# First edges of a graph layer: the sources' exponentials taken from the gathered rows, head by head, on ScalarE

## The chip, the cores and the metric

The kernel runs on one core of one Trainium2 chip. The metric is the time of one execution on the device in microseconds (us); for the kernel before it is the median of 3 runs. Engine names follow the profile: PE is the matrix engine (TensorE), DVE VectorE, ACT ScalarE, POOL GpSimd, and SP the engine that issues most plain DMAs.

## What is computed

The layer has 6250 nodes of 256 features and three parts. The change lies in the first, attention over 200,000 edges that are sorted by destination, with four heads of 64:

```
z  = einsum('ni,hid->nhd', h, W)
es = einsum('nhd,hd->nh', z, a_src)
ed = einsum('nhd,hd->nh', z, a_dst)
e  = es[src] + ed[dst];  e = where(e >= 0, e, 0.01 * e)
alpha = exp(e - max over dst) / sum over dst
out = segment_sum(alpha[:, :, None] * z[src], dst)
```

The second part (the mixer) is a linear attention over all nodes: x @ Wqkv, an exponential softmax of q and k, a 256x256 context, an output product and a norm. The third is a feed-forward part of four experts, whose gate is a second edge attention (131,072 edges). `x` plus the first two, normed, is the input of the third.

## The kernel before, in words

The exponential of a leaky sum is the larger of two products: exp(e) is max(exp(es) exp(ed), exp(0.01 es) exp(0.01 ed)), each up to a shift. So a source has eight factors, four heads by two slopes, and a destination eight; an edge's weight is the larger of two products for each head. `source_factors` and `factors_of` (L211 to L214) make the sources' ones: the largest term of each head, `most_1`, is subtracted, and two activations follow, one with a bias of 60 (`shift_c`) and one with the scale 0.01.

The program has these stages. **Head:** the nodes are normed and projected; each node's row of z with its four terms es (264 numbers, `ztab`) goes to DRAM, and the largest es of each head over all nodes becomes `most_1` (a tile of 128x4). **First edges:** the edges are laid out in 1612 chunks of 128, 33 for each tile of 128 destination nodes (28 for the last). Eight chunks are a group; there are 202 groups, the last with four chunks. **Second edges** with the feed-forward part follow, with 784 gathers from another table (L1321).

A group of first edges passes through these methods of `FirstEdges`:

- `gather` (L784, POOL): eight indirect DMAs, one for each chunk, bring 128 rows of `ztab` each into `gt` tiles of four chunks. There are seven such tiles, so three and a half groups.
- `sources` (L798, L213, L214): on DVE, for each of the two `gt` tiles, the four terms of each chunk minus `most_1`, into `src_d` (128x16); then on ACT two activations over the whole group (128x32) into `src_f`.
- `load`, `one_hot` (L807, L813), `one_hot_t` (L822), `terms` (L828, PE) and `terms_sum` (L836): the destination's factors, by a one-hot product.
- `weights` (L840, L842, DVE): the eight products and the larger of each pair, into a PSUM tile `dv`. L840 is the only reader of `src_f`.
- `weigh` (L848, DVE): the gathered rows of four chunks times the weights, in place.
- `add` (L857, PE): each chunk's one-hot matrix times its weighed rows, summed in PSUM per destination tile; a finished tile goes through `node_sums` (L766 to L768).

The order is written out by hand, in a loop over groups: gather of group g+2, `weights` and first half of `weigh` of g, `terms` of g+1, first half of `add` of g, second half of `weigh`, `one_hot` of g+1, second half of `add`, `one_hot_t` of g+2, `terms_sum` and `sources` of g+1. Between these, at six slots, `mix_hops` issues the next steps of the mixer and of the second norm (L172, L179, L883, L921, L959 to L981), which go PE, ACT, PE, DVE in turn, and at the end of each round comes one step of a sort for the second edges (L381, L383). A scheduler then places the instructions, mostly in this order, and each engine carries out its own in the order so fixed. It also adds the semaphore waits: before an instruction that reads a gathered tile, one for each of the tile's four landings; before a gather into a tile, the tile's former users.

Of the kernel before, what the change touches and what calls it, by code (L numbers as in the profile page):

```python
# [9 lines left out]
F32 = mybir.dt.float32  # L10
# [3 lines left out]
AF = mybir.ActivationFunctionType  # L14
OP = mybir.AluOpType
# [5 lines left out]
P = 128  # L21
# [6 lines left out]
G1 = 8  # L28
GH = 4
K1, K1L = 33, 28  # L30

ZW = 4 * 65
# [11 lines left out]
SHIFT = 60.0  # L44
# [15 lines left out]
def rows(t):  # L60
    return min(P, N - t * P)
# [3 lines left out]
def gps_layer(ctx: ExitStack, tc: tile.TileContext, a: dict, out: bass.AP):  # L65
    nc = tc.nc
    V, S, G, T, SP = nc.vector, nc.scalar, nc.gpsimd, nc.tensor, nc.sync
# [51 lines left out]
    ek = first.enter_context(tc.tile_pool(name="ek", bufs=1))  # L119
    pw3 = ek.tile([P, NB, 24], BF16, name="pw3")  # L120
    most_1 = ek.tile([P, 4], F32, name="most_1")


    def root(pool, var, n, w, tag):
# [70 lines left out]
    def source_max(pool, ps, m2, es, tag):  # L195

        m1 = pool.tile([P, 4], F32, name=tag + "_m1")
        V.tensor_reduce(m1, es.rearrange("p t h -> p h t"), AX.X, OP.max)
        V.tensor_copy(m2, max_over_partitions(pool, ps, m1, 4, tag))
# [12 lines left out]
    def factors_of(src_f, d, slope):  # L212
        S.activation(src_f[:, :, 0:4], d, AF.Exp, bias=shift_c)  # L213
        S.activation(src_f[:, :, 4:8], d, AF.Exp, scale=slope)  # L214

    def dest_factors(dst_f, u, ed, m2, slope):

        V.tensor_add(u[:, :, 4:8], ed, m2[:, None, :].to_broadcast([P, NT, 4]))
        V.tensor_scalar(u[:, :, 0:4], u[:, :, 4:8], 0.0, 1.0 - slope, op0=OP.min, op1=OP.mult)
        V.tensor_scalar(u[:, :, 4:8], u[:, :, 4:8], 0.0, slope - 1.0, op0=OP.max, op1=OP.mult)  # L220
        S.activation(dst_f[:, :, 0:4], u[:, :, 0:4], AF.Exp)
        S.activation(dst_f[:, :, 4:8], u[:, :, 4:8], AF.Exp, bias=shift_c)

    def in_three(parts, f, r):

        V.tensor_copy(parts[:, :, 0:8], f)
        V.tensor_sub(r, f, parts[:, :, 0:8])
        V.tensor_copy(parts[:, :, 8:16], r)
        V.tensor_sub(r, r, parts[:, :, 8:16])
        return V.tensor_copy(parts[:, :, 16:24], r)  # L230
# [268 lines left out]
    with tc.tile_pool(name="a_x", bufs=1) as ax, tc.tile_pool(name="a_w", bufs=3) as aw, tc.tile_pool(  # L499
        name="a_p", bufs=2, space=PSUM  # L500
# [242 lines left out]
    with tc.tile_pool(name="s1_w", bufs=1) as w, tc.tile_pool(name="s1_p", bufs=1, space=PSUM) as ps:  # L743
        df = q_2[:, : NT * 8].rearrange("p (t f) -> p t f", f=8)
        source_max(w, ps, most_1, es_all[:, :, 0:4], "f1")
        dest_factors(df, dl_2[:, : NT * 8].rearrange("p (t h) -> p t h", h=8), es_all[:, :, 4:8], most_1, 0.01)
        V.memset(pw3, 0.0)
        head_end = in_three(pw3[:, :NT], df, dl_2[:, : NT * 8].rearrange("p (t f) -> p t f", f=8))
    V.memset(h_all[:, NT - 1, :], 0.0)
# [20 lines left out]
    class FirstEdges:  # L770
# [20 lines left out]
        def sources(self):  # L791

            n = self.n
            d = self.w.tile([P, G1, 4], F32, name="src_d", bufs=1)
            self.sf = self.w.tile([P, G1, 8], F32, name="src_f")
            for c0 in range(0, n, GH):
                c1 = min(c0 + GH, n)
                V.tensor_sub(  # L798
                    d[:, c0:c1], self.gt[c0 // GH][:, : c1 - c0, ZW:], most_1[:, None, :].to_broadcast([P, c1 - c0, 4])
                )  # L800
            factors_of(self.sf[:, :n], d[:, :n], 0.01)

        def load(self, rows_):

# [231 lines left out]
    with tc.tile_pool(name="g1_w", bufs=2) as w, tc.tile_pool(name="g1_g", bufs=7) as gp, tc.tile_pool(  # L1036
        name="m_w", bufs=2
# [78 lines left out]
    with tc.If(many != 0):  # L1116
# [7 lines left out]
        with tc.tile_pool(name="sl_k", bufs=1) as k, tc.tile_pool(name="sl_w", bufs=1) as w, tc.tile_pool(  # L1124
            name="sl_p", bufs=1, space=PSUM
# [80 lines left out]
            for t in range(NT):  # L1206
                n, n0 = rows(t), t * P
# [30 lines left out]
    with tc.tile_pool(name="d_k", bufs=1) as dk:  # L1238
# [3 lines left out]
        with tc.tile_pool(name="d_o", bufs=1) as do:  # L1242
# [5 lines left out]
            with tc.tile_pool(name="s2_p", bufs=1, space=PSUM) as ps1:  # L1248
                room = acc2.rearrange("p t f -> p (t f)")
                source_max(do, ps1, most_2, h_all[:, :, HW:HF], "f2")  # L1250
                d = room[:, : NT * 4].rearrange("p (t h) -> p t h", h=4)
# [454 lines left out]
        with tc.tile_pool(name="g2_w", bufs=2) as w, tc.tile_pool(name="g2_g", bufs=6) as gp, tc.tile_pool(  # L1706
            name="g2_p", bufs=1, space=PSUM
# [88 lines left out]
        with tc.If(bad != 0):  # L1796

            own_edges()
            with tc.tile_pool(name="h2_k", bufs=1) as hk, tc.tile_pool(name="h2_w", bufs=1) as w, tc.tile_pool(
                name="h2_p", bufs=1, space=PSUM  # L1800
# [60 lines left out]
```

## Time and profile before

| | us |
|---|---|
| median of 3 runs | 3219.29 (3212.33 to 3220.07) |
| the profiled execution | 4023.54 |
| its span, first to last instruction | 4021.7 |
| first gather of the first edges (L784) starts | 138.1 |
| last gather of the first edges starts | 2614.0 |
| first and last gather of the second edges (L1321) | 2642.2 and 3957.9 |
| busy in the span: PE, DVE, ACT, POOL | 2498.4, 2464.6, 506.5, 2328.2 |

The profiled execution takes a quarter longer than a run. In its span there are stretches in which several engines start nothing, and many waits are put down to "remote", which means that the releaser is not in the profile.

How to read the lines. In a list of groups a line names its line of code, engine and operation, what is written and read, the shapes and a count; then the busy time and the mean duration in ns, then the idle time of the engine ahead of it and what ended most of it. In a timeline a line begins with its start and its duration, and ends, in brackets, with the idle time before it and the releaser. "issue" is idle time for which the profile shows no wait. In a list of waits a line gives who waited for whom, the sum in us, how often, and the longest. A queue entry is a wait that the engine's sequencer carries out; it is not counted as busy.

### The profile page before, as it was taken

Reading aid. Unit: us, or ns where it says so; the run is one execution under the profiler, and the core shown is the slowest. Engines: PE = TensorE matmul, PEld = TensorE weight load, DVE = VectorE, ACT = ScalarE, POOL = GpSimd, SP = SyncE. Lnnn points to the kernel's source line nnn. Section 1 sums busy time; section 2 is a strip of 40 time slices with the busy share of each in tenths; the row PEclk is TensorE's granted clock in tenths of the full one; section 3 lists DMA queues with packets and bytes.
Section 4 is the critical chain, followed back from the end, with each engine's and each line's share of the span. In section 5 each row is a group of like instructions: output and inputs, shape, how many; then the busy total and the mean of one; then the engine's idle time right before and its main releaser. Section 6 shows DMA issues by size and latency. Waiting matters only on the chain. (4 is left out here: it accounts for less than half of the span.)

```text
span 4021.7 us, 36890 instructions
## 1 busy us (share of the span) xinstructions
PE 2498.4 (62%) x10919; PEld 1773.3 (44%) x10920; DVE 2464.6 (61%) x6571; ACT 506.5 (13%) x1319; POOL 2328.2 (58%) x2436
## 2 busy tenths in 40 slices
PE   5666677755564555546555555446666767677766
PEld 4444565544443444434444433324444444444444
DVE  5566666677774776766677566625555546565657
ACT  2200011111110110111111111121111011111112
POOL 2466666665665666656666566655556556555552
PEclk8778798877776777777777777767888788888878
DMA  5443344444443443444444444332222123222221
GB/s 166 131 114 109 108 116 110 119 119 116 122 130 97 116 123 108 120 112 115 133 116 127 113 125 109 104 81 51 45 60 50 42 49 81 53 61 57 59 56 32
DMA packets 248565, 388.33 MB, mean 97 GB/s; under 512 B 73447, under 2 KB 156279, under 8 KB 248090
## 3 DMA queue, kind: packets, MB, share of 16 engines
q0 software_dynamic: 103296, 230.96, 23.1%
q1 hardware_dynamic: 142893, 154.04, 12.6%
q8 instruction: 91, 1.49, 0.1%
q14 instruction: 129, 1.05, 0.1%
q10 hardware_dynamic: 2156, 0.80, 0.1%
HBM read 345.44 MB, written 40.15 MB: 96 GB/s over the span
## 5 line engine op out<-in xcount | busy, mean ns | idle before, releaser
L784 POOL DMA_INDIRECT gt<-ztab,src_c x1612 | 1551.5, 962 | 967.3 <-issue 406.3
L857 PE MATMUL ag<-gt,oh 128*128 128x260 f32 x3224 | 1017.2, 474 | 342.6 <-DVE gt L848 232.0
L1321 POOL DMA_INDIRECT gt<-htab,src x784 | 748.6, 955 | 595.3 <-DVE dv L1390 261.2
L857 PEld LDWEIGHTS ag<-gt,oh 128*128 128x128 f32 x3224 | 754.0, 241 | 527.2 <-DVE gt L848 255.0
L1427 PE MATMUL hp<-xy,w 128*128 128x512 f32 (+1 forms) x832 | 444.3, 657 | 187.2 <-ACT hT L1432 140.5
L1447 PE MATMUL yo<-w,hT 128*128 128x256 f32 x1568 | 446.4, 425 | 111.4 <-issue 63.8
L848 DVE TENSOR_TENSOR gt<-gt,dv 128x1040 f32<-128x1040 f32 x403 | 489.0, 1224 | 13.7 <-issue 12.6
L1447 PEld LDWEIGHTS yo<-w,hT 128*128 128x128 f32 x1568 | 316.5, 209 | 246.2 <-issue 137.2
L883 PE MATMUL m<-wqkv,xy 128*128 128x256 f32 (+1 forms) x784 | 254.6, 464 | 169.5 <-DVE kmax L894 85.3
L1427 PEld LDWEIGHTS hp<-xy,w 128*128 128x128 f32 x832 | 169.0, 216 | 328.5 <-issue 167.3
L883 PEld LDWEIGHTS m<-wqkv,xy 128*128 128x128 f32 (+1 forms) x784 | 171.8, 231 | 217.2 <-DVE kmax L894 91.3
L813 DVE TENSOR_TENSOR oh<-dv,dl_c 128x1024 f32<-128x1024 f32 x202 | 244.0, 1208 | 7.8 <-PE ag L857 5.2
L1432 ACT ACTIVATE hT<-hp,b 128x512 f32<-128x512 f32 (+1 forms) x208 | 133.5, 660 | 479.4 <-remote 172.9
L1371 DVE TENSOR_TENSOR e_sel<-ed,ohq 128x384 f32<-128x384 f32 x98 | 54.1, 552 | 182.4 <-remote 136.8
L213 ACT ACTIVATE src_f<-src_d,shift_c 128x32 f32<-128x32 f32 x202 | 64.9, 321 | 772.5 <-DVE src_d L798 441.4
L381 DVE MAX8 src<-dl 128x8 f32<-128x1024 f32 x128 | 155.5, 1215 | 0.0
L383 DVE MATCH_REPLACE8 dl<-src,dl 128x1024 f32<-128x1024 f32 x127 | 153.5, 1209 | 0.0
L976 PE MATMUL m<-m_sb,qT 128*128 128x256 f32 (+1 forms) x196 | 74.4, 516 | 125.4 <-ACT qT L973 86.8
L1412 DVE TENSOR_REDUCE ag<-ag 128x40 f32<-128x120 f32 x98 | 27.2, 277 | 193.5 <-remote 154.5
L828 PE MATMUL ed<-pw,ohT 128*128 128x24 bf16 x1612 | 71.8, 176 | 106.7 <-DVE ohT L822 46.3
L828 PEld LDWEIGHTS <-ohT 128*128 128x128 bf16 x1612 | 67.1, 100 | 141.6 <-DVE ohT L822 53.6
L836 DVE TENSOR_REDUCE pw<-ed 128x64 f32<-128x192 f32 x202 | 69.6, 344 | 94.9 <-remote 74.6
(374 smaller groups left out, 2745.7 us busy)
## 6 DMA issues: line engine op xcount, KB each, us to landing
br<-rows SPq DMA_DIRECT2D x299, 256.0 KB
gt<-ztab,src_c POOLq DMA_INDIRECT x1612
gt<-htab,src POOLq DMA_INDIRECT x784
early<-ys SPq DMA_DIRECT2D x24, 512.0 KB
ys<-early SPq DMA_DIRECT2D x24, 512.0 KB
ztab<-zt SPq DMA_DIRECT2D x48, 132.0 KB
row<-in_x_dram SPq DMA_DIRECT2D x48, 128.0 KB
out_dram<-ys SPq DMA_DIRECT2D x47, 128.0 KB
```

The lines of the kernel that those rows point to most:

```text
L381: V.max(out=srtf[:, 8 * i : 8 * i + 8], in_=keyf)
L383: V.match_replace(out=keyf, in_to_replace=srtf[:, 8 * i : 8 * i + 8], in_values=keyf, imm_value=0.0)
L784: G.indirect_dma_start(out=self.gt[-1][:, c % GH, :], out_offset=None, in_=ztab[:, :], in_offset=bass.IndirectOffsetOnAxis(ap=self.idx[:, ...
L813: V.tensor_tensor(self.oh[:, :n], self.dv[:, None, :P].to_broadcast([P, n, P]), self.dl[:, :, None].to_broadcast([P, n, P]), op=OP.is_equal,)
L828: T.matmul(self.ed[:, c, :], self.ohT[:, c * P : (c + 1) * P], pw3[:, ds(self.tiles[c], 1), :].rearrange("p a b -> p (a b)"), start=True, ...
L848: V.tensor_mul(gz, gz, self.wp[:, c0:c1].unsqueeze(3).to_broadcast([P, c1 - c0, 4, 65]))
L857: T.matmul(sums[t], self.oh[:, c], self.gt[c // GH][:, c % GH, 0:ZW], start=(s0 + c == 0 or chunk_tile[s0 + c - 1] != t), stop=last,)
L883: T.matmul(out_, xy[:, t, j, :n], wqkv[:, j, c0 : c0 + D], start=(j == 0), stop=(j == 1))
L1321: G.indirect_dma_start(out=self.gt[:, c, : tab.shape[1]], out_offset=None, in_=tab[:, :], in_offset=bass.IndirectOffsetOnAxis(ap=self.idx[ ...
L1427: T.matmul(hp[:, :m], wts[e][0][:, c, j * P : (j + 1) * P], xy[:, t0 : t0 + nt, c] if m == nt * P else xy[:, t0, c, :m], start=(c == 0), s ...
L1432: S.activation(h[:, :m], hp[:, :m], AF.Gelu, bias=b1[:, e, j : j + 1])
L1447: T.matmul(yo[:n], hT[j][:, o : o + n], wts[e][1][:, j, :], start=(j == 0 and e < EARLY), stop=(j == 3))
```

## The change

The subtraction ahead of the exponentials goes. The largest terms are folded into biases, made once: `less_1` (128x8) holds 60 - most_1 for the four factors of slope 1 and -0.01 most_1 for the four of slope 0.01. In `sources`, ACT reads the terms straight from the gathered tile, at a stride of one row of 264, one activation for each tile, head and slope: 16 activations of 128x4 elements for a group instead of two of 128x32, and no DVE operation. `src_d` is gone. Nothing else is edited; `factors_of` stays in use for the second edges.

```diff
+    less_1 = ek.tile([P, 8], F32, name="less_1")
...
         dest_factors(df, dl_2[:, : NT * 8].rearrange("p (t h) -> p t h", h=8), es_all[:, :, 4:8], most_1, 0.01)
+        V.tensor_scalar(less_1[:, 0:4], most_1, -1.0, SHIFT, op0=OP.mult, op1=OP.add)
+        V.tensor_scalar(less_1[:, 4:8], most_1, -0.01, None, op0=OP.mult)
...
         def sources(self):
 
             n = self.n
-            d = self.w.tile([P, G1, 4], F32, name="src_d", bufs=1)
             self.sf = self.w.tile([P, G1, 8], F32, name="src_f")
             for c0 in range(0, n, GH):
                 c1 = min(c0 + GH, n)
-                V.tensor_sub(
-                    d[:, c0:c1], self.gt[c0 // GH][:, : c1 - c0, ZW:], most_1[:, None, :].to_broadcast([P, c1 - c0, 4])
-                )
-            factors_of(self.sf[:, :n], d[:, :n], 0.01)
+                for f in range(8):
+                    es = self.gt[c0 // GH][:, : c1 - c0, ZW + f % 4]
+                    S.activation(
+                        self.sf[:, c0:c1, f], es, AF.Exp, bias=less_1[:, f : f + 1], scale=1.0 if f < 4 else 0.01
+                    )
```

## The prediction, made before the change was run

> **What bounds the kernel now.** The page first. Its group list names the two gathers as the largest POOL work:
>
> ```profile
> L784 POOL DMA_INDIRECT gt<-ztab,src_c x1612 | 1551.5, 962 | 967.3 <-issue 406.3
> ...
> L1321 POOL DMA_INDIRECT gt<-htab,src x784 | 748.6, 955 | 595.3 <-DVE dv L1390 261.2
> ...
> L213 ACT ACTIVATE src_f<-src_d,shift_c 128x32 f32<-128x32 f32 x202 | 64.9, 321 | 772.5 <-DVE src_d L798 441.4
> ```
>
> One mean per gather (962 ns) does not say at what pace POOL can go, so the second view is the timeline of POOL alone:
>
> ```profile
> 1001.19 0.94 POOL L784 DMA_INDIRECT gt<-ztab,src_c  x1 [0.30 <-issue]
> 1002.44 0.94 POOL L784 DMA_INDIRECT gt<-ztab,src_c  x1 [0.30 <-issue]
> 1003.69 0.95 POOL L784 DMA_INDIRECT gt<-ztab,src_c  x1 [0.30 <-issue]
> ...
> 1016.21 0.94 POOL L784 DMA_INDIRECT gt<-ztab,src_c  x1 [0.30 <-issue]
> 1020.53 0.94 POOL L784 DMA_INDIRECT gt<-ztab,src_c  x1 [3.37 <-DVE qm L959]
> ```
>
> Two gathers that wait for nothing start 1.25 us apart. Over the first edges I took all start-to-start distances from the trace: 1400 of 1611 lie near 1.254, and the other 211 carry 453 us above that. At L1321, 71 distances carry 334 us more. If no gather waited, the profiled execution would be: 138 us to the first gather, 1611 x 1.254 + about 3 = 2023, 28 to the first of the second edges, 783 x 1.252 + 1 = 982, 64 to the end: 3235, with the 1.8 us around the span 3237. The profiled execution itself took 4023.54 us (span 4021.7). The median of the runs is 3219.29. So 3237 misses the median by 0.6%, and 4024 misses it by 25%: the runs look like the profile with POOL never held up. I take POOL's pace, 8 x 1.254 = 10.03 us per group of 8 chunks, as the bound of both edge stages. The consumers of a group must then need less than 10.03 us.
>
> Do they? From 440 to 2540 us the stretches show a mean of 201 us of DVE in 300, 67%. There are 201 group periods in 2466 us, 12.27 each, so DVE is busy 8.2 us a group and PE (176 of 300) 7.2. Third, the periods from one L840 to the next: taking out every gap of over 0.8 us in which DVE, ACT and PE all start nothing leaves 8.7 us, taking out only those over 1.5 us leaves 9.8. The 39 groups with no such gap have a median of 8.3. Margin under POOL: 0.2 to 1.7 us. This margin decides the case.
>
> Fourth, the step that changes, in the timeline of all engines:
>
> ```profile
> 1000.43 0.42 ACT L963 ACTIVATE kq<-kq 128x256 f32<-128x256 f32 x1 [2.71 <-DVE kq L962]
> ...
> 1004.74 0.25 DVE L798 TENSOR_TENSOR src_d<-gt,most 128x16 f32<-128x16 f32 x2
> ...
> 1005.08 0.32 ACT L213 ACTIVATE src_f<-src_d,shift_c 128x32 f32<-128x32 f32 x1 [4.23 <-DVE pw L836]
> 1005.31 0.21 ACT L214 ACTIVATE src_f<-src_d 128x32 f32<-128x32 f32 x1
> 1006.04 0.20 DVE L840 TENSOR_TENSOR pw<-pw,src_f 128x64 f32<-128x64 f32 x1
> ...
> 1022.03 0.42 ACT L963 ACTIVATE kq<-kq 128x256 f32<-128x256 f32 x1 [9.35 <-DVE kq L962]
> ...
> 1025.37 0.21 DVE L840 TENSOR_TENSOR pw<-pw,src_f 128x64 f32<-128x64 f32 x1
> ```
>
> and the waits of DVE:
>
> ```profile
> DVE pw L840 <- ACT src_f L214: 45.5, 10, 18.5
> ...
> DVE src_d L798 <- DMA gt<-ztab,src_c: 8.6, 3, 4.9
> ```
>
> ACT stands idle before L213 because it waits for the subtraction; DVE hardly waits for ACT, and in this execution hardly for a gather.
>
> **The change, part by part.**
>
> Removed, DVE: 403 subtractions (two a group, one in the last). A pair holds DVE from 1004.74 to the next start at 1004.90, 0.16 us, elsewhere 0.22: 0.19 x 202 = 38 us. What hides it: POOL's 10.03. Worth 0 while POOL bounds; without that cover 38 us.
>
> Removed, ACT: 404 activations over 32 elements, together about 0.35 us of ACT a group (0.228 from the first start to the second, 0.12 to whatever follows it).
>
> Added, ACT: 201 x 16 + 8 = 3224 activations over 4 elements, each with a bias from a tile. The nearest row is the square root over 4 elements with such a bias, L126, 297 ns by itself. For a row of them only L213 followed by another shows the distance: 0.228 us over 32 elements. The 256- and 32-element exponentials (415 and 321) are not alike in bias, so for the size I take the 297 against 321 of the bias rows: 0.228 - 0.024 = 0.204. Sixteen take 16 x 0.204 + 0.09 = 3.35 us; if nothing overlapped, 16 x 0.297 = 4.75. I take 3.35, since consecutive ones do overlap in the trace. ACT gains 3.0 us a group, 606 us in all; it was busy 36 of 300, so 1.5 us a group, and comes to 4.5 of 10.03. Not a bound; at 4.75 it would be 5.9.
>
> A rule speaks against the split: the Trainium skill, "Perfetto Trace Analysis", section Optimizing Scalar/DVE Operations, gives a fixed overhead of about 93 ns per ScalarE operation on SBUF and advises larger operations where the engine is saturated. By that figure 14 more operations are, as an estimate, 1.3 us a group; by the row they are 3.0. I use the row. With either, ACT stays far from full (at most 45%), and the time would be 3220; by the rule's figure the lateness below would halve.
>
> What is late: L840 needs the last of the sixteen. They depend on the gathers and no longer on DVE, so they can start when ACT's earlier work is done. In the first example ACT is free at 1000.85, done by 1004.2, before L840 at 1006.04: no delay. In the second it is free at 1022.45, done at 1025.8, against L840 at 1025.37: 0.4 late. Doing this comparison for all 202 groups, L840 is late in 74, on the mean over all 0.63 us; the next ACT operation is late by 0.16. Queued behind the sixteen on ACT are the mixer's copies and exponentials (L922, L963, L973, L978, L173), for which PE waits. Together 0.8 us a group, less the 0.19 of DVE: +0.6. The lower end is -0.5: L840's waits for ACT (45.5 + 17.2 of issue, 0.31 a group) vanish if the activations run early, and the 0.19. Either way 8.3 to 8.7 becomes 8.9 to 9.3, under 10.03: worth 0 here.
>
> Waits that move: the four landings of each tile, awaited by L798 (806 queue waits for 403 tiles), are now awaited by ACT, and by the in-place multiply L848 too, just where L798 stood ahead of it. A gather has to wait for ACT's reads as well: one more queue entry per tile at POOL. Its price is bounded by what POOL shows: a gather with one such entry ahead that was not held starts 1.254 us after the last, as without, and the one at L1321 with three starts after 1.249. The entries run under the gather before. I take 0; 43 ns x 403 = 17 us if one were exposed. ACT is never the tile's last reader: its reads end before L840, the PE reads that free the tile come after. So a tile comes free later by the 0.6 above at most, and the 7 tiles, 3.5 groups of gathers, cover that.
>
> A second rule bears on the removal: the skill's "GPSIMD Engine Reference", section Key points, says that GpSimd shares its SBUF interfaces with VectorE and contends with instructions of two SBUF inputs. L798 is one. By the rule at its strongest its 403 x 0.166 = 67 us could come off POOL. The row says otherwise: beside L848, 1.23 us with two SBUF inputs at 1001.79, the gathers keep 1.25. I take 0.
>
> Two small DVE operations ahead of the stage: about 0.15 each, beside the gathers that already run. End of the stage: the last group has 8 activations instead of two and a subtraction, 1.7 us against 0.7; it stands between the last landing and the second stage: +1.
>
> Sum: 0 + 0 + 0 + 1 = +1 us, in the profile's 3237 or the median's 3219: 3220.
>
> **Rivals.**
>
> A. *ACT's queue makes the consumers the bound* (slower). If the 9.8 is the true period, +0.6 gives 10.4, over 10.03 by 0.4: 201 x 0.4 = 80 us, 3300. For it: the thin margin, the cross waits PE-ACT-PE of the mixer. Against: the gaps of 1.5 us and less also contain stalls. It decides from 0.2 to 1.7 us added a group. A smaller share, in some stretches only, gives 3235 to 3300. Chance 0.32.
>
> B. *POOL is not the bound in the runs* (faster). If the 0.30 between gathers were only the recording's, consumers set the pace, and 0.5 us a group comes off: 100 us, 3120; with half of it exposed to ACT 3170. Against: the sum of 3237. Chance 0.10.
>
> C. *The activations do not run ahead*, because ACT sits behind the mixer's work or behind the landing; with POOL the bound, half of them (the first tile's) are still done before the second lands, 8 x 0.204 = 1.7 us follow: the time stays 3220. It is within the likeliest case, 0.58 together.
>
> **How the numbers follow.** About 0.3%, 10 us, is what a measurement of this kernel can tell from no change. Same 0.58 at 3212 to 3229; slower 0.32, of which some 0.06 over 3300; faster 0.10, nearly all below 3208. Range 3208 to 3300.
>
> **What would show it.** In the changed profile: L784 free starts still 1.25 apart; L798 gone, 3224 small activations about 0.2 apart; their first start not tied to DVE; waits of L840 for ACT up from 45 us but under 150; POOL's waits for PE at L784 no more than in this profile. POOL waiting for more in sum, or group periods in gap-free stretches over 10 us, proves A. Free gathers under 1.25 us apart with a shorter time prove B. The profiled execution may lengthen, as it has 2820 more records on ACT; I do not forecast it.

## The result, and the profile after

| | us |
|---|---|
| before, median of 3 runs | 3219.29 (3212.33 to 3220.07) |
| changed, median of 3 runs | 3287.79 (3281.83 to 3288.90) |
| ratio | 1.0222, 95% interval 1.0206 to 1.0237 |
| the changed kernel's profiled execution, and its span | 3281.83, 3280.0 |

The change costs 68.5 us. The forecast's likeliest case (3220, no change) is wrong. Its rival A, the consumers as the bound at 3300, is near, and the range of 3208 to 3300 holds the time.

For what follows: the profile shown of before, and all twelve experiments, come from executions in which PE's results were handed on late in many places (waits marked "remote"; the kernel before takes 3989 to 4027 us there), while the changed kernel's profile has no such wait, and the timed runs above, at 3219 and 3288 us, leave no room for them. So stage lengths are never compared between this profile and the one of before; each experiment is compared with the kernel before on its own chip. The profiles with late results also lack two thirds of the records of semaphores (that of before has 19,705, the changed kernel's 59,948), so a wait in them may be put down to a wrong releaser.

The groups of the changed kernel's page (busy time, mean ns | idle time before, and its main releaser); line numbers are up by three or four:

```profile
L787 POOL DMA_INDIRECT gt<-ztab,src_c x1612 | 1556.6, 966 | 569.4 <-issue 439.5
...
L802 ACT ACTIVATE src_f<-gt,less 128x4 f32<-128x4 f32 x3224 | 669.9, 289 | 1060.0 <-DMA gt<-ztab,src_c 880.6
L1324 POOL DMA_INDIRECT gt<-htab,src x784 | 751.6, 959 | 270.0 <-issue 209.2
```

The second edges confirm the premise: 784 gathers with 270 us of idle time ahead of them are 0.34 each, almost only the 0.30 that POOL leaves between any two. Their starts span 989.5 us, 783 x 1.264. The first edges are another picture. Their gathers start over 2107.2 us, 87 more than 1611 x 1.254, and 65 of these lie where a new tile begins, at which a gather must wait until the tile's former users are done. That is 10.46 us a group where POOL alone needs 10.03. If head, transition, second edges and end took the same in the kernel before (116, 32, 990, 36), its 3217 of span leave 2044 us for this stage, some 25 over POOL's pace. This 25 is an estimate; no profile of before without late PE results exists.

How a hold-up arises can be read in one stretch of the changed kernel's timeline of all engines. A landing is the arrival of a gather's data.

```profile
625.67 0.42 DVE L924 TENSOR_TENSOR kq<-m,kmb 128x256 f32<-128x256 f32 x1
...
629.38 1.45 ACT L802 ACTIVATE src_f<-gt,less 128x4 f32<-128x4 f32 x7 [3.43 <-DMA gt<-ztab,src_c]
...
630.73 0.35 ACT L925 COPY vt<-m 128x256 f32<-128x256 f32 x1
...
631.14 1.22 PE L886 MATMUL m<-wqkv,xy 128*128 128x256 f32 x2 [4.19 <-ACT vt L925]
...
635.44 2.79 PE L860 MATMUL ag<-gt,oh 128*128 128x260 f32 x12
635.71 0.42 DVE L924 TENSOR_TENSOR kq<-m,kmb 128x256 f32<-128x256 f32 x1 [6.50 <-PE m L886]
...
637.23 0.99 POOL L787 DMA_INDIRECT gt<-ztab,src_c  x1 [4.76 <-ACT kq L926]
```

Where the mixer's copy L925 waits for an input at all, the list of waits names DVE's L924, which here ends at 626.1. But ahead of it in ACT's queue stand activations for a later group, which wait 3.43 us for a gather to land. The copy starts at 630.73; PE has stood 4.19 us for the buffer that it frees, DVE then 6.50 for PE, and POOL 4.46 beyond its usual 0.30. The profile names ACT's L926 as POOL's releaser; by the order of the work it is rather PE's products L860, which use up the old tile and stood behind L886. There are 40 places in the stage where POOL is held by 0.1 to 4.9 us, 60 us together.

The lines of ACT's and DVE's waits (total, times, longest) that belong to this:

```profile
ACT src_f L802 <- DMA gt<-ztab,src_c: 880.6, 286, 7.2
```

```profile
DVE y_st L983 <- ACT yb L981: 94.8, 34, 6.8
...
DVE qs L969 <- ACT kq L966: 56.1, 21, 9.3
DVE n_r L133 <- ACT n_q L127: 50.9, 14, 13.7
DVE pw L843 <- ACT src_f L802: 50.4, 17, 6.8
```

ACT, which before the change came to the exponentials only after DVE's subtraction, now comes to them ahead of the gathers, and waits there. DVE waits little for the factors themselves (50 us): the last of a group's sixteen ends 11.8 us ahead of L843 (median). It waits more for the mixer's results that ACT hands on. Switching ACT between the square root and the exponential is no part of the change: both kernels load its function tables 71 times.

### The profile page after: what moved, and what is told of

Same layout as the page of the kernel before. It is cut to its first block, busy times and chain, and to the rows that moved or that the text cites. A ratio compares the mean times of both kernels' runs of the same rounds, so it can differ in the third digit from the quotient of the medians.

```text
span 3280.0 us, 40437 instructions
## 1 busy us (share of the span) xinstructions
PE 2340.5 (71%) x10919; PEld 1697.3 (52%) x10920; DVE 2425.3 (74%) x6170; ACT 1067.0 (33%) x4139; POOL 2336.6 (71%) x2436
## 5 line engine op out<-in xcount | busy, mean ns | idle before, releaser
L860 PE MATMUL ag<-gt,oh 128*128 128x260 f32 x3224 | 984.0, 462 | 211.7 <-DVE gt L851 211.1
L802 ACT ACTIVATE src_f<-gt,less 128x4 f32<-128x4 f32 x3224 | 669.9, 289 | 1060.0 <-DMA gt<-ztab,src_c 880.6
L860 PEld LDWEIGHTS ag<-gt,oh 128*128 128x128 f32 x3224 | 733.3, 235 | 377.8 <-DVE gt L851 239.8
L1450 PE MATMUL yo<-w,hT 128*128 128x256 f32 x1568 | 396.4, 396 | 52.0 <-DVE ys L1493 51.9
L1430 PE MATMUL hp<-xy,w 128*128 128x512 f32 (+1 forms) x832 | 398.5, 604 | 22.6 <-ACT hT L1435 19.4
L1450 PEld LDWEIGHTS yo<-w,hT 128*128 128x128 f32 x1568 | 291.0, 193 | 153.6 <-DVE ys L1493 77.5
L886 PE MATMUL m<-wqkv,xy 128*128 128x256 f32 (+1 forms) x784 | 246.7, 454 | 104.7 <-DVE kmax L897 63.2
L886 PEld LDWEIGHTS m<-wqkv,xy 128*128 128x128 f32 (+1 forms) x784 | 168.8, 226 | 143.4 <-DVE kmax L897 66.7
L1430 PEld LDWEIGHTS hp<-xy,w 128*128 128x128 f32 x832 | 158.6, 201 | 134.4 <-issue 104.2
L1383 DVE TENSOR_TENSOR pr<-pw,gt 128x64 f32<-128x64 f32 x98 | 22.1, 225 | 232.9 <-DMA gt<-htab,src 144.1
L1345 DVE TENSOR_TENSOR oh<-dv,dl 128x1024 bf16<-128x1024 f32 x98 | 119.0, 1215 | 0.0
L1408 PE MATMUL ag<-mq,oh 128*128 128x120 bf16 x784 | 62.0, 227 | 79.1 <-DVE mq L1403 78.8
```

The costliest lines, as they stand in the source:

```text
L802: S.activation(self.sf[:, c0:c1, f], es, AF.Exp, bias=less_1[:, f : f + 1], scale=1.0 if f < 4 else 0.01)
L860: T.matmul(sums[t], self.oh[:, c], self.gt[c // GH][:, c % GH, 0:ZW], start=(s0 + c == 0 or chunk_tile[s0 + c - 1] != t), stop=last,)
L886: T.matmul(out_, xy[:, t, j, :n], wqkv[:, j, c0 : c0 + D], start=(j == 0), stop=(j == 1))
L1430: T.matmul(hp[:, :m], wts[e][0][:, c, j * P : (j + 1) * P], xy[:, t0 : t0 + nt, c] if m == nt * P else xy[:, t0, c, :m], start=(c == 0), s ...
L1450: T.matmul(yo[:n], hT[j][:, o : o + n], wts[e][1][:, j, :], start=(j == 0 and e < EARLY), stop=(j == 3))
```

## The experiments

Three theories were tried against one another, and a fourth (W) came later. **Q**: the early place in ACT's queue, as in the stretch above. **L**: the length, sixteen operations where two were. **S**: the schedule; with other activations the scheduler gives DVE and PE another order. **W**: the waits that move when ACT reads the gathered tile. The first forecasts are in us and assume executions like the timed ones. As the experiments did not run that way, ratios to the kernel before are compared.

**The kernel before, again.** No edit.

> The kernel before, unchanged, for a profile without the stretches in which all engines stand. Both theories: about 3219 us, and POOL held in the first edges for some 25 us in sum (3217 of span less 116 to the first gather, 2020 of gathers at 1.254, 32 between the stages, 990 and 36 for the second edges and the end). Theory Q (queue): the 16 activations are placed by the scheduler up to a group early, in among the mixer's work on ACT; ACT stands there for landings, the mixer's results come late, and with them the release of the gathered tiles. Then in this run ACT should not wait for landings at all, and should reach the exponentials well after the group's last gather. Theory L (length): sixteen activations take 3.2 us where two took 0.5, and hold up L840 and the ACT work behind them.

3993.06 us, ratio 1.0008 (0.9973 to 1.0042). PE's results come late here too, so this is a second profile of the kernel before and no better one. From first to last gather start its first edges take 2422.8 us, those of the profile of before 2475.9: two profiles of one kernel differ by 53 us in this stage. Its waits of ACT and of DVE:

```profile
ACT src_f L213 <- DVE src_d L798: 443.7, 75, 24.1
```

```profile
DVE pw L840 <- ACT src_f L214: 16.6, 13, 3.1
```

**Sixteen, late.** In `sources` of the kernel before:

```diff
-            factors_of(self.sf[:, :n], d[:, :n], 0.01)
+            for c0 in range(0, n, GH):
+                c1 = min(c0 + GH, n)
+                for f in range(8):
+                    S.activation(self.sf[:, c0:c1, f], d[:, c0:c1, f % 4], AF.Exp,
+                                 bias=(shift_c if f < 4 else zero_c), scale=1.0 if f < 4 else 0.01)
```

> The kernel before with its subtraction, but with sixteen activations of 128x4 out of src_d in place of two of 128x32: the length of the change without its early place, since they still wait for DVE. Q: 3220 to 3245, ACT not waiting for landings. L: 3285 to 3305, as slow as the changed kernel or more, since the subtraction is back.

4076.05, ratio 1.0166 (1.0104 to 1.0227). Sixteen without an early place lose. This speaks against Q as the only cause; but the scheduler was free to give other orders. And L840 waits for ACT only 7.5 us in sum, less than in the kernel before, so the loss is not where L has it either.

**Four, early.** In the changed kernel, `most_1` is one maximum over all heads, copied to four columns, and:

```diff
-                for f in range(8):
-                    es = self.gt[c0 // GH][:, : c1 - c0, ZW + f % 4]
-                    S.activation(self.sf[:, c0:c1, f], es, AF.Exp, ...)
+                es = self.gt[c0 // GH][:, : c1 - c0, ZW:]
+                S.activation(self.sf[:, c0:c1, 0:4], es, AF.Exp, bias=less_1[:, 0:1])
+                S.activation(self.sf[:, c0:c1, 4:8], es, AF.Exp, bias=less_1[:, 4:5], scale=0.01)
```

> The changed kernel with one largest term for all heads, so that one activation of 128x16 does four heads: four activations a group straight from the gathered tile (some 0.9 us), free to be placed early. The early place without the length. Q: 3265 to 3290, ACT still waiting hundreds of us for landings. L: 3205 to 3222.

4053.66, ratio 1.0131 (1.0091 to 1.0171). Q's numbers are 1.014 to 1.022 of the kernel before, L's 0.996 to 1.001: this is nearly Q's, and L fails. With the run ahead of it, each theory has lost once. ACT waited for landings even longer than in the changed kernel:

```profile
ACT src_f L804 <- DMA gt<-ztab,src_c: 969.1, 221, 9.6
```

**Sixteen, in the order of the code.** In the changed kernel:

```diff
-                    S.activation(
+                    tc.keep_in_program_order(S.activation(
```

> The changed kernel, but each activation is kept behind whatever the code issues on ACT ahead of it (order alone, no wait). Same sixteen operations, no subtraction. Q: 3212 to 3235, the wait for landings nearly gone, POOL held 25 us or less. L: 3280 to 3295, as the changed kernel.

4195.85, ratio 1.0483 (1.0420 to 1.0545). Q fails here: the wait for landings fell to 213 us, and the time rose. The edge fixes ACT's order, and the scheduler answered with another order on the other engines too. So an order can cost 3% and more, and S had to be tried properly.

**The changed kernel, again.** No edit.

> The changed kernel, unchanged, beside the kernel before on one chip. In the last four runs the chip let PE stand for several us at a time (the kernel before took 3990 there), and sixteen late ones cost 1.7%, four early ones 1.3%. If length (L) and early place (Q) both cost and add up, the changed kernel is 2.5 to 3.5% over the kernel before on such a chip, and 2.2% on one where PE does not stand. If it is one of them alone, some 1.5%.

4063.58, ratio 1.0127 (1.0054 to 1.0200): length and place do not add up, though each alone seemed to cost about as much. Where PE's results come late, the change loses 1.3%, not 2.2%.

**Four, in the order of the code.** The four activations, each kept in order as above.

> One largest term for all heads, four activations of 128x16 a group, each kept behind the ACT work that the code issues ahead of it: neither length nor early place. Q: as fast as the kernel before or up to 0.5% faster. L: the same. If keeping the order of the code is itself what costs (sixteen in code order were 4.8% slower), it is 2 to 4% slower on a chip that lets PE stand.

4077.56, ratio 1.0152 (1.0100 to 1.0204). Few and late, and still slower: Q and L both fail as stated. Each of these numbers has an order of the scheduler's own making in it.

So the orders were taken out of the comparison. The order in which each engine carries out its instructions was read from the built kernel and fixed in the next by edges that order without waiting:

```diff
+def pinned(tc, nc):
+    mine = {i.name: i for i in nc.cur_bb.bb.instructions}
+    for order in PIN.values():
+        order = [n for n in order if n in mine]
+        for x, y in zip(order, order[1:]):
+            tc.add_manual_dep(mine[y], x, mybir.DependencyInfo(
+                mybir.DependencyClass.NoSync, mybir.DependencyReason.DATA), reason="pinned")
...
         for _ in steps:
             pass
+    pinned(tc, nc)
```

**New operations, old order.** `PIN` holds the kernel before's order of all five engines, sixteen where two stood.

> The changed kernel's operations with every engine's order fixed to the order that the kernel before has; the sixteen activations stand on ACT where the two stood, the subtractions are gone. Only operations and waits differ from the kernel before. A third theory joins in, S (schedule): the scheduler orders by its own idea of when things are ready, and any other set of activations gives DVE and PE another order (in the changed kernel 28% of PE's instructions and most of DVE's stand at another place), which happens to be worse; four variants that share little were all 1.3 to 1.7% slower. S: within 0.3% of the kernel before. Q: the same, since nothing stands early. L: all of the change's loss (2.2% where PE does not stand, 1.3% where it does).

4095.50, ratio 1.0155 (1.0105 to 1.0206). S and Q fail, L holds; moved waits (W) would give the same here. The trace shows the old order: PE's 10,919 matrix products stand as in the kernel before, and so do all but 9 of the 6166 DVE operations that both kernels have, where the changed kernel has 910 of them moved. L840 (here L863) waits 106.5 us for ACT; in the two profiles of the kernel before it was 45.5 and 16.6:

```profile
DVE pw L863 <- ACT src_f L822: 106.5, 43, 18.0
```

**New operations, old order, ACT free.** `PIN` without ACT.

> As the run before it, but ACT's order is left to the scheduler, which puts the activations early and in among the mixer's work; PE, DVE, POOL and SP keep the order of the kernel before. S: within 0.3% of the kernel before. Q: all of the loss (2.2% or 1.3%). L: all of the loss as well, as in the run before it.

4085.23, ratio 1.0157 (1.0117 to 1.0197), as Q and L both have it, and no more than the run ahead of it: with the other engines' order fixed, the early place changes nothing in sum. ACT stands for landings instead of for DVE:

```profile
ACT src_f L821 <- DMA gt<-ztab,src_c: 661.0, 203, 7.6
```

**Old operations, new order.** The kernel before with `PIN` from the changed kernel (PE, DVE, POOL, SP).

> The kernel before's operations, subtraction and two activations, with the order of PE, DVE, POOL and SP fixed to that of the changed kernel (each pair of subtractions behind its group's sum of terms). No activation is short, none is early. S: all of the loss (2.2% where PE does not stand, 1.3% where it does). Q and L: within 0.3% of the kernel before.

4008.65, ratio 0.9983 (0.9960 to 1.0006). S is out: the changed kernel's order is as good as the old one. The run also shows that fixing the order of these four engines costs nothing by itself; fixing ACT's as well made no difference between the two runs ahead of it.

**Four, old order.** The four activations of before, every engine in the kernel before's order.

> One largest term for all heads, four activations of 128x16 a group straight from the gathered tile, no subtraction; the order of every engine is fixed to that of the kernel before, the four stand where the two stood. The fixed orders before showed that the loss is neither the schedule nor the early place alone. Left are L (sixteen operations at the old place hold up L840) and a theory W (waits): reading the gathered tile on ACT moves four landings per tile to ACT and to the weighing, and adds a queue entry per tile at POOL. L: 0.995 to 1.003 of the kernel before. W: all of the loss, 1.013 to 1.016.

4008.62, ratio 1.0065 (1.0038 to 1.0092). Between L and W: against the 1.55% of the sixteen (measured on another chip, each against the kernel before there), 0.9 is gone with twelve of them, and 0.65% stays although DVE is spared the subtractions. L840's wait for ACT is back at what it was before:

```profile
DVE pw L864 <- ACT src_f L825: 46.6, 18, 21.3
```

What is left may be the moved waits, or that four operations take 0.9 us where two took 0.44; this was not taken apart.

**Sixteen from `src_d`, old order.** The late sixteen, every engine in the kernel before's order.

> The subtraction stays and sixteen activations of 128x4 read src_d; the order of every engine is fixed to that of the kernel before. Waits at DVE and POOL are those of the kernel before; only the number of activations differs. L: 1.012 to 1.018. W: 0.998 to 1.004.

4059.35, ratio 1.0168 (1.0125 to 1.0211). L holds, W as the main cause is out: here the waits at DVE and POOL are those of the kernel before.

```profile
DVE pw L868 <- ACT src_f L826: 190.5, 82, 14.6
```

The starts and ends alone, without the semaphores, say the same: L840 starts within 0.05 us of the end of its last activation in 127 of 201 groups, in the kernel before run again in 30.

**Thirty-two, old order.** `for _ in range(2):` around the activation: each result is computed twice.

> The changed kernel with every activation carried out twice into the same place, in the fixed order of the kernel before: 6.6 us of ACT a group where the sixteen take 3.3. The suspected cost doubled, the waits for landings and the POOL entries the same. L: 1.03 to 1.06, since nothing of the second 3.3 us can hide. W: 1.015 to 1.02.

4359.34, ratio 1.0935 (1.0889 to 1.0982), more than L expected. L840 waits for ACT in 142 of 202 groups:

```profile
DVE pw L864 <- ACT src_f L823: 715.8, 142, 15.8
```

But more was added than the 3.3 us of the forecast. Here are sixteen in the changed kernel's timeline, and the thirty-two in this run's timeline of ACT:

```profile
1014.25 3.16 ACT L802 ACTIVATE src_f<-gt,less 128x4 f32<-128x4 f32 x16
```

```profile
1010.63 8.51 ACT L823 ACTIVATE src_f<-gt,less 128x4 f32<-128x4 f32 x32
```

Two activations into the same place start 0.32 us apart, the second after the first has ended; two into different places 0.21. So the waits and the POOL entries are those of the sixteen, but the added work is 5.35 us.

The ratios put these runs on one scale: as a share of the kernel before's time, over 201 group periods, four cost 0.13 us a group, sixteen from the tile 0.31, sixteen from `src_d` 0.33, thirty-two 1.86. (The lengths of the stage in single profiles can't serve, since they differ by 0.26 us a group for one kernel.) On ACT the two took 0.44 us. Of the first 2.7 us added a ninth shows, of the next 5.35 over a quarter: much of the second sixteen hides too, against L's forecast, but less of it, as the slack between ACT and L840 is mostly used up.

No version tried beats the kernel before.

## Why the prediction's likeliest case was wrong, step by step

- **POOL's pace as the bound of both stages**: right for the second edges, which run at it; in the first edges it is only the floor. Unheld gathers start 1.254 us apart in the changed kernel (median of the first edges). Rival B, which had free gathers under 1.25 us apart and a gain, is not what happened. That the sum of 3237 met the median was in part luck: its head, transition and end (138, 28 and 64 us) came from an execution with late results; the changed kernel's profile has 116, 32 and 36. With these, POOL never held up comes to some 3191, an estimate 28 us under the median. So the kernel before was held already.
- **Costs of the operations**: right. Sixteen at 0.204 us each were to take 3.35 us. The changed kernel's timeline has them in 3.16, and the stretch

```profile
1040.00:1340.00 300.00, 189.57 (x837) 144.44 (x836) 231.22 (x472) 120.08 (x511) 221.34 (x230) 0.80 0.50 138
```

  (PE, weight loads, DVE, ACT, POOL busy in 300 us) gives ACT 120.08, 4.2 us in a group of 10.46, where 4.5 was forecast. Sixteen in place of two add 2.7 us a group, nearer to the row's 3.0 than to the rule's 1.3.
- **Nothing comes off POOL with the subtraction**: right, but by a row that doesn't bear on it. The second input of L848, `dv`, lies in PSUM, so it has only one in SBUF. L798 and L840 have two there: in the profile of before, unheld gathers that overlap one of them are followed by the next after 1.262 us on the mean, others after 1.255, at most 2 us in all. A gather took 962 ns before and takes 966 in the changed kernel.
- **The extra queue entries at POOL cost nothing**: not contradicted. POOL's entries rose from 537 to 933, and the gathers that are not held keep 1.254; in sixteen from `src_d`, without the extra entries, the loss is as large.
- **+0.6 us a group for the consumers**: the right sign, but about twice too much, as far as the time shows it. The timed runs lost 0.34 us a group (68.5 over 201 periods); where PE's results come late, the changed kernel run again lost 0.25 and the one with orders fixed 0.31.
- **"Either way 8.3 to 8.7 becomes 8.9 to 9.3, under 10.03: worth 0 here"**: this is the step that failed. The 8.7 came from taking out every stretch of over 0.8 us in which DVE, ACT and PE start nothing. But an engine that starts nothing may be at work, as DVE is here in the timeline of before:

```profile
1020.37 1.23 DVE L848 TENSOR_TENSOR gt<-gt,dv 128x1040 f32<-128x1040 f32 x1
1020.53 0.94 POOL L784 DMA_INDIRECT gt<-ztab,src_c  x1 [3.37 <-DVE qm L959]
1021.52 0.42 DVE L962 TENSOR_TENSOR kq<-m,qm 128x256 f32<-128x256 f32 x1
```

  From 1020.37 to 1021.52 the rule takes out 1.15 us in which L848 runs. Counted again over the whole profile of before, taking out the stretches in which the three start nothing leaves 8.6 us a group; taking out those of over 0.8 us in which all three stand idle leaves 9.9. The changed kernel's profile, which has no late results to remove, loses 1.29 of its 10.47 us by the first count and 0.34 by the second. So the margin under POOL was at most some 0.1 us and not 1.3, and the 0.3 that was added doesn't fit under it. Measured: 10.46 us a group and 3287.79. Rival A, with 9.8 + 0.6 = 10.4 and 3300, named the right kind of loss, but that its sum comes so near is in part luck: the 9.8 stands against an estimated 10.15 for the stage in the kernel before, and the 0.6 against 0.3.
- **Buffers of 3.5 groups cover a lateness**: only while POOL is the slower side on average. In the changed kernel ACT waits for landings 286 times and POOL is held for tiles at 40 places, in the same stage: the two sides take turns at being late, and the seven tiles don't even it out.
- **The mixer behind the activations**: named, but sized at 0.16 us a group from the next ACT operation of the old trace. That comparison left the order as it was. The scheduler moved the activations about a group ahead, where they wait for landings with the mixer behind them; the three largest waits of DVE for the mixer's and norm's ACT results (94.8, 56.1, 50.9) are 202 us. In the kernel before run again the first of these stands at 81.7 already, the other two under 1. All of DVE's waits for ACT between 140 and 2500 us are 102 us there and 199 in the changed kernel run again. The fixed orders show that this place is not the root: with the activations at the old place, a loss of the same size comes with longer waits of L840 instead.

That the sixteen cost is shown where PE's results come late (sixteen from `src_d`, old order). For the timed runs it is carried over, since no variant ran without late results. What stays open: the split of their 2.2% between length and place; why sixteen, late, lost as much without making L840 wait; why the order of the code costs 3% beyond the fixed old order with the same sixteen operations; and what of the 0.65% of the four activations is due to the moved waits.

## What to carry to other kernels

Count an operation that is moved to an idle engine by the latency that its consumer sees, not by the engine's load: in sixteen from `src_d` ACT was busy for a third of the stage (689.5 of 2060 us), and with the order of all engines fixed the sixteen short activations in place of two still cost 1.7%. Before calling a step hidden, size the margin with work and real waits between engines left in; a stretch in which nothing starts is no stall while an engine is running. Where two readings of the margin differ by more than the step, the forecast is open. And a step that no longer waits for a late engine may be placed early by the scheduler, where the wait for its own inputs holds up the work behind it, as the 880.6 us of ACT's waits for landings show.

## What the runs showed of the hardware

The same kernel took 3219 us in the timed runs and 3989 to 4027 us on the chips of the experiments, with the gathers' unheld pace the same (1.251 to 1.254 us). The difference shows mainly in waits for PE's results, which arrive up to microseconds after PE's modelled end: in the trace of before a product (L883) is recorded to end at 1014.33 us, and L959, which reads it, starts at 1020.03 after 5.18 us of idle time for which the profile has no other releaser. The mean granted clock was 0.78 in that profile and 0.85 in the changed kernel's. What delays the results isn't in the profile. Activations over 4 elements took 289 ns each, 0.19 us from start to start, whether they read at a stride of 264 elements or from a compact tile (287 to 290). Two in a row into the same place started 0.32 us apart.
